# Separate tiles for messages and weighted values, reversed matmul order, and a query copy in a two-network graph kernel

## The chip, the cores and the metric

The kernel runs on one core of a Trainium2 chip. The metric is the device time of one launch in microseconds. A core has five engines that work side by side, each through its own queue in the order of the program: TensorE (PE, with its weight loads shown as PEld), VectorE (DVE), ScalarE (ACT), GpSimd (POOL) and SyncE (SP). An instruction that needs another engine's or a transfer's result waits for a semaphore, and everything behind it in the same queue waits too. Row gathers are issued by POOL, all other transfers that matter here by SP.

## The reference

A graph of N = 3125 nodes with 256 features has 53125 edges (`src`, `dst`), sorted by `dst`. Two networks follow each other, each added to its input and normalised:

```
h = x;  for each of 2 attention layers:
    q, k, v = h@wq+bq, h@wk+bk, h@wv+bv            # 4 heads of 64
    alpha   = sum(q[dst]*k[src]) / 8                # per edge and head
    alpha   = softmax of alpha over the edges of a dst
    h       = segment_sum(v[src]*alpha, dst) + h@ws + bs
    h       = leaky_relu(batch_norm(h))
x = layernorm(x + h)
h = x;  for each of 3 relational layers:
    msg = relu(h[src] * (edge_attr @ nn_w.T + nn_b))
    out = h@root + bias
    for r in 0..2: out += (mean of msg over a dst's edges of type r) @ W[r]
    h = out
out = layernorm(x + h)
```

## The kernel before

Edges, padded to 53248, lie in T = 416 tiles of 128, one edge per partition. A group is G = 8 tiles, and there are NG = 52 groups. A prologue prepares index tables and the first table of keys and values, then a branch leads to `sorted_edges` (its other side, for unsorted edges, is not taken). The order within each engine's queue is the order in which the Python program writes the instructions (`tc.manual_schedule()`). Tiles come from pools with a number of buffers; a new tile waits until the last reader of the buffer's former tile is done.

`gather` (L442) is one indirect transfer on POOL that fetches 128 rows by the indices `src_c`. Each pass over the edges has 416 of them, and there are five passes: two in `window_attention`, three in `window_relational`.

**Attention.** A loop over `it` from 0 to 51 is a software pipeline: in iteration `it`, `loads(it+3)` sends the query window of a later group (SP), `penalties(it+1)` and `windows(it+1)` prepare the next one (`windows` compares destinations with a ramp on DVE, L511), `queries` (L520, PE) spreads query rows to edges, `logits(it)` multiplies by the gathered keys and sums per head (L525, L527, DVE), `turn(it-1)` (L532, PE) and `maxima(it-2)` (two scans, L537 and L538, DVE) make running maxima, `less(it-2)` (L544 and L546, PE) subtracts them, `weights(it-2)` (L550) and `weigh(...)` (L558, ACT) take the exponential and scale the values, in place in the gathered tile `kvg`. `nodes_of(it-3)` (L568) makes eight one-hot tiles that tell each edge's node, `sums(it-4)` (L575, PE) multiplies them with the weighted values and `add(it-5)` (L586, DVE) adds the result to a per-node accumulator. `rows(it+2)` issues eight gathers at the end of an iteration. Once a block of nodes is complete, `finish` divides by the softmax's sum (L612), adds the skip product (`skip`, L617 and L619) and keeps the result (L623). After the loop the last three groups are drained, with one-hot tiles made on POOL (`nodes_of(..., GP)`) and part of the weighting on DVE (`weigh_rest`, L563). This drain is called a tail below. Then come batch statistics and, after the first layer, the projection of the second layer's keys and values (L418), or, after the second, the layer norm that writes the rows for the relational part.

**Relational.** A loop over `s` from 0 to 103 takes half a group, a four of tiles, per step. `rows` gathers a group ahead by four groups into `xs`, a ring of six groups; `edge_weights` (L943, PE) computes the edge factors, `messages` (L961 on DVE, then the ReLU L962 on ACT) works in place in `xs`; a column of ones behind each row of `xs` counts edges in the first layer. `keys` (L953) makes one-hot tiles of node and edge type, `products` (L969, PE) reduces four tiles in PSUM and `add` (L983) adds them to a ring of node blocks. A complete block goes through `node`: means (L997, and the block's reset L998), transposes (`turn`, L1012 and L1013), the product with four weight matrices (`product`, L1023) and the sum with the bias (L1028), which SP writes to the table for the next layer. A new layer's first gather waits until all rows of that table are written.

Of the kernel before, what the change touches and what calls it, by code (L numbers as in the profile page):

```python
# [8 lines left out]
F32 = mybir.dt.float32  # L9
# [3 lines left out]
AF = mybir.ActivationFunctionType  # L13
OP = mybir.AluOpType
# [4 lines left out]
P = 128  # L19
# [4 lines left out]
D = 256  # L24
H = 4
HD = D // H
HC = HD + 1
# [431 lines left out]
def window_attention(tc, A, h_tab, L):  # L459
# [7 lines left out]

    with tc.tile_pool(name="a1", bufs=1) as one, tc.tile_pool(name="kvf", bufs=6) as kp, \
            tc.tile_pool(name="a3", bufs=3) as sp, tc.tile_pool(name="a2", bufs=2) as sp2, \
# [13 lines left out]

        kvs, qws, lds, pns, ohts, qds, fs, ws, ohs, pos, tos = ({} for _ in range(11))


        def loads(n, g):
            ldb = sp.tile([P, 2 * P], F32, name="ldb")
            SY.dma_start(ldb, view(L["ld_d"], g * G * P, [[2 * P, 4], [0, W2], [1, 2 * P]]))
            qw = sp.tile([P, D], F32, name="qw")  # L490
            _, at = nc.values_load_multi_w_load_instructions(
                L["q_row"][:, g * 4:g * 4 + 4], engines=[SY.engine], min_val=0, max_val=N + 3,
                skip_runtime_bounds_check_because="a pair's first dst: a node, or one of the padding's")
            for a in range(4):
                SY.dma_start(qw[a * W2:(a + 1) * W2, :], q_tab[bass.ds(at[a], W2), :])
            lds[g], qws[g] = ldb, qw

# [11 lines left out]
        def windows(g):  # L509
            oht = sp2.tile([P, 2, P], F32, name="oht")  # L510
            V.tensor_scalar(oht.rearrange("p k e -> p (k e)"), lds.pop(g), L["wid"], None, op0=OP.is_equal)  # L511
            ohts[g] = oht

# [28 lines left out]
        def less(g):  # L542

            TE.matmul(less_p, ident, al[:, g * G + 1:g * G + G + 1, :].rearrange("p t h -> p (t h)"),  # L544
                      start=True, stop=False)
            TE.matmul(less_p, fs.pop(g)[:, 64:64 + P], neg, start=False, stop=True)  # L546

# [5 lines left out]
        def weigh(g, a, b):  # L553

            for j in range(a, b):
                for q in range(H):
                    c = kvs[g][:, j, D + q * HC:D + (q + 1) * HC]
                    S.activation(c, c, AF.Copy, scale=ws[g][:, j * H + q:j * H + q + 1])  # L558

        def weigh_rest(g, a):  # L560

            c = kvs[g][:, a:, D:].rearrange("p t (h c) -> p t h c", h=H)
            V.tensor_tensor(c, c, bc(ws[g][:, a * H:].rearrange("p (t h) -> p t h", h=H), 3, HC), op=OP.mult)  # L563

# [6 lines left out]
        def sums(g):  # L571
            oh, kv = ohs.pop(g), kvs.pop(g)
            po = qps.tile([P, AC], F32, name="pof")
            for j in range(G):
                TE.matmul(po, oh[:, j, :], kv[:, j, D:], start=(j == 0), stop=(j == G - 1))  # L575
            pos[g] = po
# [24 lines left out]
        def finish(i):  # L601
# [12 lines left out]
            def skip(p):  # L614
                for c in range(2):
                    for k in range(2):
                        TE.matmul(p[:, c, :], wqs[:, k, D + c * P:D + (c + 1) * P], xT[:, k, blk],  # L617
                                  start=(k == 0), stop=False)
                    TE.matmul(p[:, c, :], q["a"][:, c * P:(c + 1) * P], ident, start=False, stop=True)  # L619

            def keep(p):
                for c in range(2):
                    S.activation(xT[:, c, blk], p[:, c, :], AF.Identity, bias=cols[:, 0, c:c + 1])  # L623
# [252 lines left out]
def window_relational(tc, A, first, out, L):  # L876
# [8 lines left out]
    h = L["xT"].rearrange("p k n -> p (k n)")[:KM].rearrange("p (i c) -> p i c", c=D)  # L885
    NQ, XB, AB = 2 * NG, 6, 3

    with tc.tile_pool(name="rx", bufs=1) as one, tc.tile_pool(name="edf", bufs=3) as sp, \
            tc.tile_pool(name="atf", bufs=4) as wp, tc.tile_pool(name="rnf", bufs=2) as np_, \
            tc.tile_pool(name="edpf", bufs=2, space=PSUM) as ps, \  # L890
# [3 lines left out]
        rc = one.tile([KM, KT], F32, name="rck")  # L894
        xs = one.tile([P, XB, G, KW], F32, name="xsf")
        ab = one.tile([P, AB, G, 64], F32, name="abf")
        at_d = L["dram"].tile([NG, P, 4 * P], F32, name="at_d")
        V.memset(ab, 0.0)
        V.memset(ab[:, :, :, DD], 1.0)
        V.memset(xs[:, :, :, D], 1.0)  # L900

        ats, ohs, ews, pps, tos = {}, {}, {}, {}, {}

# [42 lines left out]
        def rows(g, table):  # L946
            for j in range(G):
                gather(xs[:, g % XB, j, :D], table[:, :], L["src_c"][:, g * G + j:g * G + j + 1])

# [6 lines left out]

        def messages(q):
            g, u = divmod(q, 2)
            x4 = xs[:, g % XB, 4 * u:4 * u + 4, :D]
            xk = x4.rearrange("p (a k) c -> p k a c", k=2)  # L960
            V.tensor_tensor(xk, ews.pop(q), xk, op=OP.mult)  # L961
            S.activation(x4, x4, AF.Relu)  # L962

        def products(n, q):
            g, u = divmod(q, 2)
            wide = D + (n == 0)
            pp = ps.tile([P, 2 * D], F32, name="ppf")[:KM, :KW]
            for j in range(4 * u, 4 * u + 4):
                TE.matmul(pp[:, :wide], ohs[g][:, j, :], xs[:, g % XB, j, :wide],  # L969
                          start=(j == 4 * u), stop=(j == 4 * u + 3))  # L970
            pps[q] = pp
# [13 lines left out]
        def node(n, i, nxt, w, bias):  # L985
# [18 lines left out]
            def turn(c):  # L1004
                if q["end"]:
                    if c == 0:
                        q["t"] = ps.tile([P, 2, 2, D], F32, name="ewf")
                    t = q["t"][:, c].rearrange("p a d -> p (a d)")
                else:
                    t = ps1.tile([P, 2 * D], F32, name="nodf")  # L1010
                for b in range(3):
                    TE.transpose(t[:, b * KM:(b + 1) * KM], q["k"][:, b, c * P:(c + 1) * P], ident[:KM, :KM])  # L1012
                TE.transpose(t[:, 3 * KM:4 * KM], h[:, i, c * P:(c + 1) * P], ident[:KM, :KM])  # L1013
                S.copy(q["m"][:, c, :R].rearrange("p r (b k) -> p b r k", b=3),
                       t[:, :3 * KM].rearrange("p (b r k) -> p b r k", b=3, r=R))
                S.copy(q["m"][:, c, R], t[:, 3 * KM:4 * KM])

            def product():
                pool, name = (ps, "ppf") if i == NT - 1 else (ps1, "nodf")
                q["o"] = pool.tile([P, 2 * D], F32, name=name)[:KM, :D]  # L1020
                for c in range(2):
                    for r in range(R + 1):
                        TE.matmul(q["o"], q["m"][:, c, r, :], w[:, r, c, :], start=(r + c == 0),  # L1023
                                  stop=(r == R and c == 1))

# [36 lines left out]
        for n in range(3):  # L1062
# [5 lines left out]
            for s in range(NQ):  # L1068
# [8 lines left out]
                if s + 1 < NQ:  # L1077
                    edge_weights(s + 1)
                messages(s)
                if s >= 2:  # L1080
# [693 lines left out]
```

## Time and profile before

| what | us |
|---|---|
| median of 9 runs (2959.47 to 2967.19) | 2965.18 |
| the profiled execution's own time | 2972.51 |
| its span | 2970.7 |
| mean granted TensorE clock | 0.876 |
| PE busy | 2473.0 (83%) |
| DVE busy | 2181.1 (73%) |
| POOL busy | 2032.5 (68%) |
| ACT busy | 1341.8 (45%) |
| 1248 relational gathers, busy | 1202.6 |
| 832 attention gathers, busy | 799.6 |

Busy time is the time in which an engine executes at least one instruction. "Idle before" a group of instructions is time in which its engine stood still directly ahead of them; the profile names what ended it, and "issue" where it sees nothing that was waited for. The chain is the sequence of work that ended last, followed back from the end. A group of a stretch's instructions is written as: start, duration, engine, line, operation, tiles written and read, shapes, number of instructions merged, and in brackets the idle time before it.

### The profile page before, as it was taken

How to read it: one execution, taken by the hardware profiler on the slowest of the kernel's cores; microseconds unless marked ns; L12 is line 12 of the kernel's file. 1: busy time of each engine (PE TensorE's matmuls, PEld its weight loads, DVE VectorE, ACT ScalarE, POOL GpSimd, SP SyncE). 2: the span in 40 equal slices, each digit the busy share in tenths (PEclk: the TensorE clock that was granted, in tenths of full speed). 3: DMA queues.
4: the chain of work that ended last, by engine and by line, in shares of the span. 5: the costliest groups of instructions: out<-in, count | busy, mean ns of one | idle time of the engine just before them, and what ended most of it. 6: DMA issues, size and time to landing. Idle time of an engine off the chain costs nothing.

```text
span 2970.7 us, 45198 instructions
## 1 busy us (share of the span) xinstructions
PE 2473.0 (83%) x12210; PEld 1823.8 (61%) x12210; DVE 2181.1 (73%) x5167; ACT 1341.8 (45%) x4207; POOL 2032.5 (68%) x2131
## 2 busy tenths in 40 slices
PE   6688888887888788849899988788898878988887
PEld 3366666663666666636667766466666656666665
DVE  5599999975899999866666665566666646777775
ACT  1388787861788788653332332122222212222222
POOL 0677777744777777537777775777777757777774
PEclk9688888887888888859999999799999979999998
DMA  4788888836888888555555553444444444444442
GB/s 131 236 263 247 247 243 242 238 101 216 252 245 247 245 240 242 163 160 163 150 149 147 147 150 103 138 140 139 135 131 140 131 124 132 147 139 147 137 145 84
DMA packets 290315, 517.96 MB, mean 174 GB/s; under 512 B 101389, under 2 KB 170394, under 8 KB 290054
## 3 DMA queue, kind: packets, MB, share of 16 engines
q0 software_dynamic: 126720, 383.94, 44.8%
q1 hardware_dynamic: 162902, 130.81, 14.5%
q8 instruction: 104, 1.70, 0.2%
q14 instruction: 158, 1.29, 0.1%
q10 hardware_dynamic: 431, 0.21, 0.0%
HBM read 468.08 MB, written 46.70 MB: 173 GB/s over the span
## 4 chain that ended last, share of the span: by engine, by line
PE 43%; DVE 17%; DMA 16%; issue 12%; POOL 9%; DVEq 1%; ACT 1%; SPq 0%; POOLq 0%; another core or an unknown queue 0%; ACTq 0%
PE ppf L969 14%; PE ewf L943 8%; DMA xsf<-h_tab,src_c 8%; POOL kvg L442 8%; PE nodf L1023 6%; DMA kvg<-kv_tab,src_c 6%; PE pof L575 4%; DVE xsf L961 3%; DVE kvg L525 2%; DVE ohkf L953 2%; PE qdf L520 2%; POOL xsf L442 2%; PE qdf L418 1%; PE partps L617 1%; DVE ohn L568 1%
## 5 line engine op out<-in xcount | busy, mean ns | idle before, releaser
L442 POOL DMA_INDIRECT xsf<-h_tab,src_c x1248 | 1202.6, 964 | 488.0 <-issue 274.6
L442 POOL DMA_INDIRECT kvg<-kv_tab,src_c x832 | 799.6, 961 | 325.1 <-issue 219.2
L558 ACT ACTIVATE kvg<-kvg,wts 128x65 f32<-128x65 f32 x3216 | 786.3, 336 | 3.5
L962 ACT ACTIVATE xsf<-xsf 128x1024 f32<-128x1024 f32 x312 | 329.9, 1058 | 1008.2 <-DVE xsf L961 1008.1
L961 DVE TENSOR_TENSOR xsf<-ewf,xsf 128x1024 f32<-128x1024 f32 x312 | 381.5, 1223 | 527.1 <-DMA xsf<-h_tab,src_c 322.1
L969 PE MATMUL ppf<-xsf,ohkf 128*126 128x256 f32 (+1 forms) x2496 | 702.3, 429 | 0.0
L969 PEld LDWEIGHTS ppf<-xsf,ohkf 128*126 128x126 f32 x2496 | 494.4, 208 | 182.3 <-issue 41.0
L943 PE MATMUL ewf<-nnwf,atw 33*128 33x256 f32 x2496 | 383.5, 430 | 163.2 <-DVE xsf L961 162.0
L575 PE MATMUL pof<-kvg,ohn 128*128 128x260 f32 x1664 | 434.6, 419 | 6.9 <-DVE ohn L568 3.2
L575 PEld LDWEIGHTS pof<-kvg,ohn 128*128 128x128 f32 x1664 | 338.1, 209 | 106.2 <-ACT kvg L558 22.6
L943 PEld LDWEIGHTS ewf<-nnwf,atw 33*128 33x128 f32 x2496 | 230.9, 200 | 272.7 <-DVE xsf L961 211.7
L525 DVE TENSOR_TENSOR kvg<-qdf,kvg 128x1024 f32<-128x1024 f32 x208 | 252.0, 1211 | 63.9 <-DMA kvg<-kv_tab,src_c 33.0
L1023 PE MATMUL nodf<-rwt,mts 128*126 128x256 f32 x1152 | 264.8, 383 | 0.0
L953 DVE TENSOR_SCALAR ohkf<-iotas,kr_c 128x126 f32<-128x126 f32 x1248 | 260.5, 295 | 0.0
L527 DVE TENSOR_REDUCE alf<-kvg 128x16 f32<-128x1024 f32 x208 | 253.8, 1220 | 7.1
L1023 PEld LDWEIGHTS nodf<-rwt,mts 128*126 128x126 f32 x1152 | 220.7, 192 | 34.3
L520 PE MATMUL qdf<-qw,oht 32*128 32x256 f32 x1664 | 201.3, 505 | 24.2 <-DVE kvg L525 8.6
L532 PE MATMUL soft<-identf,alf 128*32 128x128 f32 x312 | 59.0, 303 | 169.0 <-DVE fmax L537 163.9
L568 DVE TENSOR_SCALAR ohn<-iotas,nr_c 128x128 f32<-128x128 f32 x800 | 169.6, 300 | 0.0
L520 PEld LDWEIGHTS qdf<-qw,oht 32*128 32x128 f32 x1664 | 127.4, 239 | 67.9 <-issue 22.6
L983 DVE SCALAR_TENSOR_TENSOR kacc<-ppf,k_high,kacc 126x256 f32 (+1 forms) x312 | 151.2, 485 | 11.1
L550 ACT ACTIVATE wts<-soft 128x32 f32<-128x32 f32 x104 | 20.5, 198 | 295.9 <-PE soft L546 294.3
(223 smaller groups left out, 2148.8 us busy)
## 6 DMA issues: line engine op xcount, KB each, us to landing
atw<-at_d SPq DMA_DIRECT2D x104, 256.0 KB
xsf<-h_tab,src_c POOLq DMA_INDIRECT x1248
kvg<-kv_tab,src_c POOLq DMA_INDIRECT x832
ldb<-ld_rows SPq DMA_DIRECT2D x104, 128.0 KB
qw<-q_tab SPq DMA_DIRECT2D x416, 32.0 KB
at_d<-atw SPq DMA_DIRECT2D x52, 256.0 KB
abf<-in_edge_attr_dram SPq DMA_DIRECT2D x51, 128.0 KB
q_tab<-qs SPq DMA_DIRECT2D x50, 128.0 KB
```

Of the source, the lines that this page charges most:

```text
L442: return GP.indirect_dma_start(out=dst, out_offset=None, in_=table, in_offset=rows_of(idx))
L520: TE.matmul(qd[:, a, k, :], ohts[g][r, k, :], qws[g][r, :], start=True, stop=True)
L525: V.tensor_mul(kv, qds.pop((g, u)).rearrange("p a k c -> p (a k) c"), kv)
L527: V.tensor_reduce(al[:, t:t + 4, :], kv.rearrange("p t (h c) -> p t h c", h=H), AX.X, OP.add)
L558: S.activation(c, c, AF.Copy, scale=ws[g][:, j * H + q:j * H + q + 1])
L575: TE.matmul(po, oh[:, j, :], kv[:, j, D:], start=(j == 0), stop=(j == G - 1))
L943: TE.matmul(ew[:, k, a, :], ats[g][r, 2 * u + a, :], nnw[r, :], start=True, stop=True)
L953: V.tensor_scalar(oh[:, j, :], iota[:, :KM], L["kr_c"][:, g * G + j:g * G + j + 1], None, op0=OP.is_equal)
L961: V.tensor_tensor(xk, ews.pop(q), xk, op=OP.mult)
L962: S.activation(x4, x4, AF.Relu)
L969: TE.matmul(pp[:, :wide], ohs[g][:, j, :], xs[:, g % XB, j, :wide], start=(j == 4 * u), stop=(j == 4 * u + 3))
L1023: TE.matmul(q["o"], q["m"][:, c, r, :], w[:, r, c, :], start=(r + c == 0), stop=(r == R and c == 1))
```

## The change

- `messages` writes into a tile `msf` of its own (four buffers) and no longer in place; the ones come from a constant by a small ACT copy, in the first layer only. The gathered rows lie in twelve tiles `xsf` of four rows each instead of a ring of six groups, without the extra column.
- `weigh` and `weigh_rest` write into a tile `wvg` (two buffers) instead of in place in `kvg`, and `sums` reads it. `kvg` has five buffers instead of six.
- `sums`, `products`, `turn`, `product` and `keep` take their tiles, columns or relations last to first. `skip` starts with the divided block, `less` with the maxima, `turn` with the node's own row.
- `windows` copies the query rows on DVE into `qwc`, from which `queries` reads; `loads` sends the four transfers in reverse.

```diff
-            tc.tile_pool(name="kvf", bufs=6) as kp, \
+            tc.tile_pool(name="kvf", bufs=5) as kp, \
...
-            for a in range(4):
+            for a in reversed(range(4)):
                 SY.dma_start(qw[a * W2:(a + 1) * W2, :], q_tab[bass.ds(at[a], W2), :])
...
             V.tensor_scalar(oht.rearrange("p k e -> p (k e)"), lds.pop(g), L["wid"], None, op0=OP.is_equal)
-            ohts[g] = oht
+            qw = sp2.tile([P, D], F32, name="qwc")
+            V.tensor_copy(qw, qls.pop(g))
+            ohts[g], qws[g] = oht, qw
...
+            TE.matmul(less_p, fs.pop(g)[:, 64:64 + P], neg, start=True, stop=False)
             TE.matmul(less_p, ident, al[:, g * G + 1:g * G + G + 1, :].rearrange("p t h -> p (t h)"),
-                      start=True, stop=False)
-            TE.matmul(less_p, fs.pop(g)[:, 64:64 + P], neg, start=False, stop=True)
+                      start=False, stop=True)
...
+            if a == 0:
+                wvs[g] = sp2.tile([P, G, AC], F32, name="wvg")
...
-                    S.activation(c, c, AF.Copy, scale=ws[g][:, j * H + q:j * H + q + 1])
+                    S.activation(wvs[g][:, j, q * HC:(q + 1) * HC], kvs[g][:, j, D + q * HC:D + (q + 1) * HC], AF.Copy,
+                                 scale=ws[g][:, j * H + q:j * H + q + 1])
...
-            for j in range(G):
-                TE.matmul(po, oh[:, j, :], kv[:, j, D:], start=(j == 0), stop=(j == G - 1))
+            for j in reversed(range(G)):
+                TE.matmul(po, oh[:, j, :], kv[:, j, :], start=(j == G - 1), stop=(j == 0))
...
                 for c in range(2):
+                    TE.matmul(p[:, c, :], q["a"][:, c * P:(c + 1) * P], ident, start=True, stop=False)
                     for k in range(2):
                         TE.matmul(p[:, c, :], wqs[:, k, D + c * P:D + (c + 1) * P], xT[:, k, blk],
-                                  start=(k == 0), stop=False)
-                    TE.matmul(p[:, c, :], q["a"][:, c * P:(c + 1) * P], ident, start=False, stop=True)
+                                  start=False, stop=(k == 1))
...
         def rows(g, table):
-            for j in range(G):
-                gather(xs[:, g % XB, j, :D], table[:, :], L["src_c"][:, g * G + j:g * G + j + 1])
+            for q in (2 * g, 2 * g + 1):
+                xs[q] = xp.tile([P, 4, D], F32, name="xsf")
+                for j in range(4):
+                    gather(xs[q][:, j, :], table[:, :], L["src_c"][:, q * 4 + j:q * 4 + j + 1])
...
+        def messages(n, q):
+            ms[q] = wp.tile([P, 4, KW], F32, name="msf")
+            m = ms[q][:, :, :D]
+            by_rows = [x.rearrange("p (a k) c -> p k a c", k=2) for x in (m, xs.pop(q))]
+            V.tensor_tensor(by_rows[0], ews.pop(q), by_rows[1], op=OP.mult)
+            if n == 0:
+                S.copy(ms[q][:, :, D:], one4)
+            S.activation(m, m, AF.Relu)
...
-            for j in range(4 * u, 4 * u + 4):
-                TE.matmul(pp[:, :wide], ohs[g][:, j, :], xs[:, g % XB, j, :wide],
-                          start=(j == 4 * u), stop=(j == 4 * u + 3))
+            for j in reversed(range(4)):
+                TE.matmul(pp[:, :wide], ohs[g][:, 4 * u + j, :], ms[q][:, j, :wide], start=(j == 3), stop=(j == 0))
...
-                for b in range(3):
+                TE.transpose(t[:, 3 * KM:4 * KM], h[:, i, c * P:(c + 1) * P], ident[:KM, :KM])
+                for b in (2, 1, 0):
                     TE.transpose(t[:, b * KM:(b + 1) * KM], q["k"][:, b, c * P:(c + 1) * P], ident[:KM, :KM])
-                TE.transpose(t[:, 3 * KM:4 * KM], h[:, i, c * P:(c + 1) * P], ident[:KM, :KM])
...
-                for c in range(2):
-                    for r in range(R + 1):
+                for c in (1, 0):
+                    for r in reversed(range(R + 1)):
```

## The prediction

> **What bounds the kernel now.** I read the stages first, then the gathers, then what stands between the stages. The cuts of the first view are at the first and last row gather of each pass; its columns are length, then busy time (and instructions) of PE, PEld, DVE, ACT and POOL, then granted clock, DMA share and GB/s.
>
> ```profile
> 89.43:616.61 527.18, 429.38 (x2293) 326.84 (x2294) 469.40 (x965) 403.05 (x1659) 400.67 (x416) 0.83 0.84 246
> 616.61:700.65 84.04, 73.70 (x250) 43.91 (x248) 57.81 (x145) 29.09 (x84) 12.97 (x17) 0.96 0.26 96
> 700.65:1226.10 525.45, 426.16 (x2286) 326.54 (x2287) 467.96 (x961) 400.70 (x1657) 398.94 (x416) 0.83 0.84 245
> ...
> 1303.64:1833.35 529.71, 471.80 (x2379) 350.62 (x2380) 346.71 (x882) 169.05 (x248) 403.23 (x416) 0.91 0.56 156
> ...
> 1861.20:2387.90 526.70, 450.24 (x2160) 329.16 (x2161) 332.45 (x825) 133.74 (x195) 400.22 (x416) 0.91 0.45 136
> ...
> 2411.50:2937.10 525.60, 452.31 (x2154) 328.33 (x2155) 365.43 (x935) 141.43 (x217) 399.09 (x416) 0.90 0.48 142
> ```
>
> Five passes, two of attention and three relational, take 526 to 530 us each, although their work on PE, DVE and ACT differs widely. What they share is POOL: 416 gathers. A few of those, in attention and in a relational pass:
>
> ```profile
> 303.84 0.94 POOL L442 DMA_INDIRECT kvg<-kv_tab,src_c  x1 [0.30 <-issue]
> ...
> 305.09 0.95 POOL L442 DMA_INDIRECT kvg<-kv_tab,src_c  x1 [0.30 <-issue]
> ...
> 2003.12 1.01 POOL L442 DMA_INDIRECT xsf<-h_tab,src_c  x1 [0.30 <-issue]
> 2004.44 0.94 POOL L442 DMA_INDIRECT xsf<-h_tab,src_c  x1 [0.30 <-PE ppf L969]
> ```
>
> A gather starts every 1.25 us: 0.945 of work and 0.305 before the next. In the waits of POOL inside the passes none is longer than 0.3, whatever engine is named: POOL never stands still for data or a buffer. So a pass costs 416 x 1.25 = 520 us and the 6 to 10 us by which some gathers are longer than 0.945 (the profile's mean is 0.961 and 0.964). PE at 80 to 90% busy is in its shade. The other 335 us are the start (89), the two attention tails (84 and 78), the ends of relational passes (28 and 24) and the last tail (34). A change pays or costs only through the gather's period, or through the chain in a tail.
>
> Does a wait cost POOL time? Semaphore instructions at the gather line, first pass and then the relational ones:
>
> ```profile
> L442 POOLq EVENT_SEMAPHORE  x46: 17/17/17, 145.4 to 600.6; - x46
> ...
> L442 POOLq EVENT_SEMAPHORE  x1176: 17/17/34843, 1356.9 to 2928.9; - x196
> ```
>
> Nearly every relational gather has a second wait and needs an extra instruction of 17 ns; in attention 46 of 416 have one. The idle time between gathers is 0.30 in both. It lies inside that gap.
>
> **The change part by part**, as the instructions are ordered in both kernels.
>
> *Messages in their own tiles.* L962 and the products now use msf, and gathers wait for DVE's product instead of PE's. Gathers that wait on PE (1169 of 1248) become 298 that wait on DVE. Gain on POOL 0, by the comparison above. In the first relational pass 104 four-column copies on ACT are new: 0.27 us each by the small copies at L1016, 28 us, on an engine busy 169 of 530 us, placed while it waits for DVE (it waits 1008 us there). Cost 0; with that cover gone, 0.27 us at the end of that pass.
>
> *Products last to first.* Relational: one activation makes the four tiles, so nothing is later; 1248 products lose their gather wait. Of L575's 832 matmuls, 104 groups keep one waiting matmul each; the profile has 824 semaphore instructions of 56 ns on PE's queue there, 46 us. All this lies under POOL's period. In the tails the chain's pof groups take 3.51 us for 8 matmuls, 0.44 each, as they do without a break, so removed waits give 0 (end of the range: 2 us gained, some 0.4 in each of five tails).
>
> The reverse order has a price in attention: the first matmul of `sums` needs the last one-hot tile. In steady groups that delays PE by about 1.4 us (DVE's eight tiles take 1.7 to 1.9 us) but PE then waits for DVE anyway: 169 us before L532 in all, 3.4 us in the group at 304.5. Hidden, as long as DVE is no earlier. In the tails it shows. First tail:
>
> ```profile
> 618.51 12.97 POOL L568 TENSOR_SCALAR ohn<-iotas,nr_c 128x128 f32<-128x128 f32 x16 [1.90 <-PE pof L575]
> ...
> 631.23 3.67 PE L575 MATMUL pof<-kvg,ohn 128*128 128x260 f32 x16
> ```
>
> POOL's sixteen tiles end at 631.48, and PE began the group of the last eight at 631.23. POOL itself waited for the sums of group 47, whose first matmul (612.53) came 0.8 before its last tile was done (611.64 + 1.65 = 613.29); their end slips by 0.5 to 0.8, so POOL's end does, and the group starts at about 632.2: +1.0. Second tail, the same pattern:
>
> ```profile
> 1239.67 6.83 POOL L568 TENSOR_SCALAR ohn<-iotas,nr_c 128x128 f32<-128x128 f32 x8 [8.23 <-PE soft L532]
> ...
> 1245.86 1.48 PE L575 MATMUL pof<-kvg,ohn 128*128 128x260 f32 x6
> ```
>
> Group 48's sums slip 0.7, POOL's eight tiles end at 1247.2, PE starts at 1247.3 instead of 1245.86: +1.4.
>
> *`skip` with the divided block first.* In both tails PE had done one `wqs` pair before the division was ready and now does it behind it:
>
> ```profile
> 641.91 0.49 PE L619 MATMUL qdf<-identf,naf 128*128 128x128 f32 x2 [1.54 <-DVE naf L612]
> ...
> 642.23 0.61 PE L617 MATMUL qdf<-xT,wqs 128*128 128x128 f32 x4
> ```
>
> Half of an x4 group moves behind the wait, twice 0.22: +0.5 in each tail. Tails together: 1.0 + 1.4 + 0.5 + 0.5 = **+3.4 us**. Bounds: 0 if another wait already covers it, 6 if each of the three last `sums` in each tail slips a whole one-hot series less what is done (about 1.0). In `less`, L546 goes ahead of L544; the pair's end moves by 0.2 us in front of an activation with 4.6 us idle: 0. `keep` in reverse: before, too, the first activation waited for all of PE's group: 0.
>
> *Relational `turn` and `product`.* After the last DVE mean come three transposes instead of two: +0.15 us (0.49 for three) at three pass ends, **+0.4** (-0.5 to +1). The final product starts at 2404.50, its copies end at 2401.88, so needing the last copy first costs 0.
>
> *Queries copied on VectorE.* 104 new copies 128x256. The nearest row is L511, same shape, next instruction in the queue:
>
> ```profile
> L511 DVE TENSOR_SCALAR oht<-ldb,wid x104: 329/343/558, 108.9 to 1213.5; 128x256 f32<-128x256 f32 x104
> ```
>
> The next DVE instruction follows 0.26 us later (302.82 to 303.08), so 52 x 0.26 = 14 us of DVE per pass. DVE is busy 469 of 527 and spends the rest on waits and issue; attention's first group lags its gather by 20 us, which shrinks to 3 to 5 us by the middle of the pass, with idle moments from there on. Taking 0.26 off each idle moment in turn, the lag at the pass's end grows by 0.3 at most: 0 (up to +3). Behind the copy in the queue stand the accumulation, `logits` and so PE's next queries. The copy also waits for four query DMAs; they are issued two groups (20 us) ahead, and the SP queue sends them earlier than before, since the buffer is now freed by the copy, a group earlier than by PE. Only the first group of a pass has no lead: about 0.3 us, no gather waits for it. PE's L520 loses its 416 DMA waits, under the same shade.
>
> The copy can hold the gathers, though. In attention they exceed 0.945 us by 16 ns x 832 = 13.3 us. DVE instructions with one SBUF source that stand beside them are L568 and L511, 169.6 + 37.7 = 207 us busy, so 0.064 us held per us. The copies add some 37 us of that kind: **+2.4 us**. Upper bound: each holds POOL for its whole 0.26, 104 x 0.26 = 27. Lower bound: -3, since moved DVE work can also miss the gathers. I take 2.4, from the nearest rows.
>
> The Trainium skill speaks against this copy: SBUF — State Buffer, section Who interferes with whom, says that an fp32 copy from SBUF to SBUF uses both ports and that GpSimd, which generates such gathers' descriptors, blocks until it ends. By that rule taken whole the copies would cost up to 104 x 0.34 = 35 us (an estimate from the page and L511's duration), and the sum would be 39 instead of 6.2. L511, which that section puts in the same class, has not stopped gathers for anything near its length here.
>
> *Five buffers.* A gather into group g+5's tile now waits for ACT's weighting of group g (before: g+6's for its sums). ACT ends group 0 at 139.3 and the gather of group 5 would start at 141.0: 1.7 us spare, at most 1.3 of which the first copies and `less` use; later groups have 4 to 20 us. 0 (up to +1). The weighted tile has two buffers; its reuse waits for sums that PE does ahead of `less`, for which the weighting waits anyway: 0.
>
> **Sum:** 3.4 + 0.4 + 2.4 = +6.2 us. The profiled execution took 2972.51 us (span 2970.7 and 1.8 around it), 7.3 above the median of 2965.18; 2972.5 becomes 2978.7, the median **2971.4**, x1.0021. Measuring this kernel tells about 0.2% (5.9 us) from no change, so it stands at the edge.
>
> **Rivals.**
> 1. *Copies hold the gathers for their length* (for: L998, 0.56 us, is often beside gathers of 1.2 us; against: L511). 27 instead of 2.4: 2996; half of it 2983.
> 2. *DVE becomes attention's bound.* For: busy 89% with long chains. It needs over 0.5 us per group, twice the copy; at 0.6, with the lag's catch-up spent, +5 per pass: 2981.
> 3. *Faster, by gathers that are held less.* Gathers lose 13.3 us in attention and 19 ns x 1248 = 23.7 us in the relational passes. Message rows are now 1024 bytes apart instead of 1028 on arrival, so DVE's steps can shift against the gathers. If half of 23.7 goes, -12: 2959.5. It decides for not slower from 6.2 us, for over 0.2% faster from 12.1 us. Against: nothing there removes a DVE instruction.
> 4. *Nothing changes*: tails covered, copies harmless: 2965.
> 5. *PE paces, and 2500 waits fewer pay.* L969 has 429 ns and L1023, without waits, 383: 46 x 2496 = 115 us, 2850. Against: POOL's even 1.25 us. 1 in 50.
>
> **Numbers.** Forecast (+1 to +12) 0.48, about half of it over 5.9; rival 1 0.16, rival 2 0.08, rival 3 0.17 (0.13 of it beyond 0.2%), rival 4 0.09, rival 5 0.02. Slower 0.48 x 0.52 + 0.24 = 0.49; faster 0.15; same 0.36. The range takes in rival 3's half and most of rival 1: 2954 to 2992; the forecast's own is 2966 to 2977.
>
> **What would show it.** Passes of 526 to 531 us with a gap of 0.30; attention gathers at a mean of 0.963 to 0.967; attention tails 86 and 79 to 80 us; PE's first `sums` matmul after the last one-hot tile. A wait over 0.3 on POOL inside a pass, or attention gathers above 0.98, makes it wrong.

## The result and the profile after

The changed kernel takes 2971.67 us (median of 10 runs, 2967.14 to 2981.8) beside 2964.54 us for the kernel before (31 runs): ratio 1.0032, 95% interval 1.0024 to 1.0040. The medians differ by 7.1 us; the ratio, which is taken over all runs, makes it 9.5 us (7.1 to 11.9). The forecast was 2971.4, slower by about 0.2%. The profiled execution took 2976.4 us (span 2974.6), 4.7 above its median, while that of the kernel before was 8.0 above its own. Two spans that differ by 3.9 us while the medians differ by 7.1 warn that one profile of each can't settle where 7 us went. So I read the places here, and the sizes from eight more profiles further down.

The stages of the changed kernel, cut at the first and last row gather of each pass (columns as in the prediction's first view):

```profile
90.53:621.24 530.71, 421.87 (x2290) 317.60 (x2291) 480.58 (x1017) 401.60 (x1654) 401.72 (x416) 0.83 0.84 245
621.24:707.49 86.25, 76.06 (x252) 44.12 (x251) 57.97 (x145) 28.98 (x88) 11.81 (x17) 0.94 0.25 93
707.49:1235.23 527.74, 415.75 (x2278) 311.55 (x2279) 477.22 (x1013) 400.93 (x1653) 401.30 (x416) 0.85 0.84 244
1235.23:1313.34 78.11, 42.35 (x191) 32.95 (x189) 57.96 (x152) 40.79 (x108) 11.26 (x18) 0.72 0.28 86
1313.34:1841.78 528.44, 455.56 (x2379) 342.52 (x2380) 347.07 (x882) 178.41 (x352) 402.00 (x416) 0.93 0.58 156
...
1869.30:2393.86 524.56, 442.39 (x2156) 326.06 (x2157) 333.05 (x825) 133.47 (x195) 398.15 (x416) 0.91 0.46 137
...
2419.18:2943.28 524.10, 448.49 (x2162) 328.68 (x2163) 366.36 (x935) 141.09 (x217) 397.66 (x416) 0.90 0.48 142
```

The attention passes grew by 3.5 and 2.3 us and their tails by 2.2 and 0.6; the three relational passes shrank by 1.3, 2.1 and 1.5. The page's gather groups (busy, mean ns of one, idle before):

```profile
L442 POOL DMA_INDIRECT xsf<-h_tab,src_c x1248 | 1197.8, 960 | 488.9 <-issue 399.3
...
L442 POOL DMA_INDIRECT kvg<-kv_tab,src_c x832 | 803.0, 965 | 329.0 <-issue 227.3
```

And the semaphore instructions at the gather line:

```profile
L442 POOLq EVENT_SEMAPHORE  x427: 17/17/35112, 87.1 to 2931.2; - x143
```

832 attention gathers took 803.0 us instead of 799.6. The semaphore instructions fell from 1293 to 427 (all of the run), and the gap between two gathers stayed 0.30: removing the waits paid nothing, as costed. One gap is not 0.30. The timeline of ACT and POOL there, before and then after the change:

```profile
131.54 7.78 ACT L558 ACTIVATE kvg<-kvg,wts 128x65 f32<-128x65 f32 x32
...
140.04 0.95 POOL L442 DMA_INDIRECT kvg<-kv_tab,src_c  x1 [0.31 <-issue]
```

```profile
135.23 7.78 ACT L561 ACTIVATE wvg<-kvg,wts 128x65 f32<-128x65 f32 x32
...
139.51 0.94 POOL L442 DMA_INDIRECT kvg<-kv_tab,src_c  x1 [0.30 <-issue]
...
143.28 0.94 POOL L442 DMA_INDIRECT kvg<-kv_tab,src_c  x1 [2.83 <-ACT wvg L561]
```

The gather at 143.28 is the first of group 5. It waits until ACT has weighted group 0 (135.23 + 7.78 = 143.01), because with five buffers it writes into group 0's tile. The prediction saw 1.7 us to spare here, with that gather at 141.0. In the kernel before the first gather of group 5 starts at 140.04 and ACT ends group 0 at 139.32 (131.54 + 7.78), so the spare was 0.7: the row that the prediction took is the gather after it.

The two places in the tails that the prediction priced, after the change:

```profile
625.23 11.81 POOL L572 TENSOR_SCALAR ohn<-iotas,nr_c 128x128 f32<-128x128 f32 x16 [3.99 <-issue]
...
637.09 3.77 PE L579 MATMUL pof<-wvg,ohn 128*128 128x260 f32 x16
...
1250.05 6.49 POOL L572 TENSOR_SCALAR ohn<-iotas,nr_c 128x128 f32<-128x128 f32 x8 [7.50 <-PE soft L534]
...
1256.59 3.77 PE L579 MATMUL pof<-wvg,ohn 128*128 128x260 f32 x16
```

PE begins these sums when POOL's last one-hot tile is complete (625.23 + 11.81 = 637.04; 1250.05 + 6.49 = 1256.54), as the reversed order requires; before, it began 0.25 and 0.64 us ahead of that. Counted from the last gather of the pass, it begins 1.2 and 1.6 us later than before (15.85 for 14.62, 21.36 for 19.76); the prediction had 1.0 and 1.4.

### The profile page after: what moved, and what is told of

The parts are those of the page before. It is cut to its first block, busy times and chain, and to the rows that moved or that the text cites. A ratio compares the mean times of both kernels' runs of the same rounds, so it can differ in the third digit from the quotient of the medians.

```text
span 2974.6 us, 43134 instructions
## 1 busy us (share of the span) xinstructions
PE 2428.4 (82%) x12210; PEld 1786.6 (60%) x12210; DVE 2203.6 (74%) x5271; ACT 1350.4 (45%) x4311; POOL 2029.7 (68%) x2131
## 4 chain that ended last, share of the span: by engine, by line
POOL 21%; DMA 20%; DVE 19%; issue 19%; PE 17%; ACT 3%; DVEq 1%; SPq 0%; POOLq 0%; another core or an unknown queue 0%; ACTq 0%
DMA xsf<-h_tab,src_c 11%; POOL xsf L442 11%; POOL kvg L442 10%; DMA kvg<-kv_tab,src_c 6%; PE ppf L977 4%; DVE ohkf L959 4%; DVE kacc L990 3%; ACT wvg L561 2%; PE ewf L947 2%; DVE kvg L527 2%; PE nodf L1030 2%; PE pof L579 2%; DVE msf L967 1%; PE qdf L418 1%; DVE ohn L572 1%
## 5 line engine op out<-in xcount | busy, mean ns | idle before, releaser
L442 POOL DMA_INDIRECT kvg<-kv_tab,src_c x832 | 803.0, 965 | 329.0 <-issue 227.3
L561 ACT ACTIVATE wvg<-kvg,wts 128x65 f32<-128x65 f32 x3216 | 786.4, 336 | 3.6
L970 ACT ACTIVATE msf<-msf 128x1024 f32<-128x1024 f32 x312 | 330.0, 1058 | 990.5 <-DVE msf L967 988.1
L967 DVE TENSOR_TENSOR msf<-ewf,xsf 128x1024 f32<-128x1024 f32 x312 | 381.4, 1222 | 516.1 <-DMA xsf<-h_tab,src_c 366.5
L977 PE MATMUL ppf<-msf,ohkf 128*126 128x256 f32 (+1 forms) x2496 | 687.3, 423 | 0.6 <-DVE rsr L1049 0.5
L977 PEld LDWEIGHTS ppf<-msf,ohkf 128*126 128x126 f32 x2496 | 484.3, 204 | 178.0 <-issue 41.8
L579 PE MATMUL pof<-wvg,ohn 128*128 128x260 f32 x1664 | 446.2, 427 | 87.8 <-DVE ohn L572 63.9
L579 PEld LDWEIGHTS pof<-wvg,ohn 128*128 128x128 f32 x1664 | 347.1, 214 | 189.0 <-issue 81.8
L959 DVE TENSOR_SCALAR ohkf<-iotas,kr_c 128x126 f32<-128x126 f32 x1248 | 261.9, 296 | 0.1
L522 PE MATMUL qdf<-qwc,oht 32*128 32x256 f32 x1664 | 170.1, 477 | 27.0 <-DVE qwc L513 18.6
L572 DVE TENSOR_SCALAR ohn<-iotas,nr_c 128x128 f32<-128x128 f32 x800 | 168.9, 299 | 0.0
L990 DVE SCALAR_TENSOR_TENSOR kacc<-ppf,k_low,kacc 126x256 f32 (+1 forms) x312 | 148.4, 476 | 9.7 <-PE ppf L977 8.9
L522 PEld LDWEIGHTS qdf<-qwc,oht 32*128 32x128 f32 x1664 | 108.0, 223 | 63.2 <-issue 22.6
```

What stands on the lines that cost most here:

```text
L442: return GP.indirect_dma_start(out=dst, out_offset=None, in_=table, in_offset=rows_of(idx))
L522: TE.matmul(qd[:, a, k, :], ohts[g][r, k, :], qws[g][r, :], start=True, stop=True)
L561: S.activation(wvs[g][:, j, q * HC:(q + 1) * HC], kvs[g][:, j, D + q * HC:D + (q + 1) * HC], AF.Copy, scale=ws[g][:, j * H + q:j * H + q + 1])
L579: TE.matmul(po, oh[:, j, :], kv[:, j, :], start=(j == G - 1), stop=(j == 0))
L959: V.tensor_scalar(oh[:, j, :], iota[:, :KM], L["kr_c"][:, g * G + j:g * G + j + 1], None, op0=OP.is_equal)
L967: V.tensor_tensor(by_rows[0], ews.pop(q), by_rows[1], op=OP.mult)
```

## Experiments

Four sets, each timed beside the kernel before on the same chip. There the kernel before took 2965.04, 3655.95, 2964.75 and 2974.48 us; only ratios within a set are compared.

### Undoing parts of the change

Without the copy (`e1_no_copy`):

```diff
-            qw = sp2.tile([P, D], F32, name="qwc")
-            V.tensor_copy(qw, qls.pop(g))
-            ohts[g], qws[g] = oht, qw
+            ohts[g], qws[g] = oht, qls.pop(g)
```

> The changed kernel with the DVE copy of the queries taken out (queries read the four transfers' tile again); all else as changed. Theory A (the copy costs twice: it holds gathers, and as it waits for all four query transfers it delays DVE in the first two groups, which with five buffers blocks one gather for 2.83 us): that block goes, the attention gathers lose 13 to 14 us over 0.945 instead of 16.8, the median falls by about 6 us, 2971.7 to 2965 to 2966. Theory B (only the block is real, the gathers' 3.4 us is scatter of one profile): -2.8, about 2969. Theory C (five buffers block the gather whatever the copy does): the wait on ACT near 143 stays, change of the median under 1 us.

Measured: 2970.14 us, ratio 1.0015 (1.0005 to 1.0025). The gathers lose 14.1 us (800.3 of page time less 832 x 0.945), as theory A said, but the time didn't fall to its 2965 to 2966: without the copy the change still costs 4.4 us (1.5 to 7.4). The wait is still there, shorter:

```profile
138.65 0.94 POOL L442 DMA_INDIRECT kvg<-kv_tab,src_c  x1 [1.58 <-ACT wvg L559]
```

So the copy isn't its only cause. The first queries show another. In the kernel before PE started them 20.4 us after the first gather (109.79 - 89.43). Here, without any copy, it starts them 22.9 after (109.87 - 87.00). Before, then without the copy:

```profile
109.79 3.97 PE L520 MATMUL qdf<-qw,oht 32*128 32x256 f32 x16 [8.56 <-DVE oht L511]
```

```profile
109.87 2.11 PE L520 MATMUL qdf<-qw,oht 32*128 32x256 f32 x16 [9.52 <-DMA qw<-q_tab]
```

The four query transfers are sent in reverse, and PE's first matmul needs the one sent last. In the changed kernel DVE's copies delay the first multiplication further:

```profile
112.03 0.29 DVE L513 COPY qwc<-qw 128x256 f32<-128x256 f32 x1 [2.13 <-DMA qw<-q_tab]
...
117.10 0.29 DVE L513 COPY qwc<-qw 128x256 f32<-128x256 f32 x1 [2.05 <-DMA pn<-pen_rows]
117.40 1.22 DVE L527 TENSOR_TENSOR kvg<-qdf,kvg 128x1024 f32<-128x1024 f32 x1
```

The first multiplication stands behind the copy of group 1, before which DVE waits for a transfer (the profile names that of `pn`): it starts 26.9 us after the first gather (117.40 - 90.53), without the copy 25.7 (112.67 - 87.00), before the change 24.9 (114.35 - 89.43).

Direct reading in the first two groups only (`e2_direct_first`):

```diff
-            qw = sp2.tile([P, D], F32, name="qwc")
-            V.tensor_copy(qw, qls.pop(g))
+            qw = qls.pop(g)
+            if g > 1:
+                qc = sp2.tile([P, D], F32, name="qwc")
+                V.tensor_copy(qc, qw)
+                qw = qc
```

> The changed kernel, but the first two groups of each layer read the query transfers directly, and the other 50 still go through the copy. Theory A: the 2.83 us block at 143 goes, because DVE's first multiplication is back at 25 us after the first gather instead of 27; the gathers stay held by 16 to 17 us in the two attention passes; median -2.8, about 2969. Theory B: the same here. Theory C: the block stays, no change. If later copies also add lag, the block shrinks but some of it stays.

Measured: 2974.29 us, ratio 1.0036 (1.0023 to 1.0049; five runs). The wait shrank to 0.96 us, another of 1.08 us came at 168, and the gathers stayed at 802.9 us. The time didn't fall, so the runs give no sign that the wait in the first groups is what the change costs.

Sums and `skip` in the old order (`e3_forward`):

```diff
-            for j in reversed(range(G)):
-                TE.matmul(po, oh[:, j, :], kv[:, j, :], start=(j == G - 1), stop=(j == 0))
+            for j in range(G):
+                TE.matmul(po, oh[:, j, :], kv[:, j, :], start=(j == 0), stop=(j == G - 1))
```

> The changed kernel with sums first to last again and with skip's products in the old order. Theory A (the reversed order costs in the tails what the last one-hot tile is late): the two attention tails fall from 86.3 and 78.1 to about 84 and 77.5, passes unchanged, median -2.8 us, about 2969. Rival (the tails' difference lies elsewhere, in the copy or in the clock that PE was granted): tails stay at 86 and 78, change under 1 us.

Measured: tails 84.0 and 76.3 us as theory A said, but 2972.77 us, ratio 1.0034 (1.0022 to 1.0046; six runs). The interval doesn't exclude the 2.8 us, but gives no sign of them.

### One part alone

The relational part alone (`e4_rel_only`), the kernel before up to `window_relational` and the changed one from there:

```diff
-        xs = one.tile([P, XB, G, KW], F32, name="xsf")
...
+                xs[q] = xp.tile([P, 4, D], F32, name="xsf")
...
+            ms[q] = wp.tile([P, 4, KW], F32, name="msf")
```

> The kernel before with the relational part of the change alone (messages in a tile of their own, rows in twelve tiles 1024 bytes apart, products, turn and product in the new order). Theory A (gathers there are really held less: 18.5 us in the three passes instead of 23.2, and the end is 2 us shorter): -5 us against the kernel before, about 2959.5, ratio 0.998. Rival (scatter of one profile, the part is worth nothing): ratio 1.000 within 0.0005. Rival (the transposes' order costs in the gaps): +0.4.

Measured: 2965.96 us, ratio 1.0002 (0.9993 to 1.0011): no gain. Its relational gathers lose 20.3 us (1199.7 less 1248 x 0.945); the two other kernels with the old relational code that ran at the usual pace and left it alone lose 19.1 and 19.8. The profile of before, with 23.2, was the odd one.

The three attention parts alone ran first on a chip on which the kernel before took 3655.95 us, at a granted clock of 0.81 instead of 0.88. Why this chip is slower stays open.

Copy alone (`f1_copy_only`, and again as `g1_copy_only`):

```diff
+            qw = sp2.tile([P, D], F32, name="qwc")
+            V.tensor_copy(qw, qls.pop(g))
+            ohts[g], qws[g] = oht, qw
...
-            for a in range(4):
+            for a in reversed(range(4)):
```

> The kernel before, with the queries' copy on DVE and the reversed order of their four transfers alone; six buffers as before. Theory A (each copy holds a gather a little): the attention gathers lose 14 to 17 us over 0.945 instead of 10 to 13, no wait over 0.3 on POOL, since six buffers cover the late first groups; +3 to +4 us, ratio 1.0010 to 1.0014. Rival 1 of the prediction at half length: +13, ratio 1.0045. Rival (the copies are free and the loss lies in the buffers and the tails): under +1, ratio 1.000.

Measured there: 3656.66 us, ratio 1.0006 (0.9990 to 1.0023).

Orders alone (`f2_order_only`):

```diff
-            for j in range(G):
-                TE.matmul(po, oh[:, j, :], kv[:, j, D:], start=(j == 0), stop=(j == G - 1))
+            for j in reversed(range(G)):
+                TE.matmul(po, oh[:, j, :], kv[:, j, D:], start=(j == G - 1), stop=(j == 0))
```

> The kernel before, in place and with six buffers, with the attention's orders alone: sums last to first, skip and less with their late operand first, keep in reverse. Theory A: attention tails 86 and 78 to 79.5 instead of 84 and 76.5 to 77.5, passes unchanged, +3, ratio 1.0010. Rival (the waits removed from PE pay somewhere in the passes): ratio 0.999 or below. Rival (the tails only scatter): 1.000.

Measured there: 3716.47 us, ratio 1.0152 (1.0126 to 1.0179), with attention passes of 699 and 692 us against 663 and 658 with the copy alone. None of the expectations had that.

Tiles and five buffers alone (`f3_tiles_only`, and again as `g2_tiles_only`):

```diff
-            tc.tile_pool(name="kvf", bufs=6) as kp, \
+            tc.tile_pool(name="kvf", bufs=5) as kp, \
...
+                wvs[g] = sp2.tile([P, G, AC], F32, name="wvg")
```

> The kernel before, with five buffers for the gathered groups and the weighted values in a tile of their own, alone: no copy, sums forward. Theory A (five buffers block a gather near the start of the first attention pass even without the copy, 1.6 us in the run without copies): one or two waits on ACT over 0.3, 1 to 2 us together; +1 to +2, ratio 1.0005. Rival (ACT writing to another tile holds the gathers as well): attention gathers lose 16 us or more, +5. Rival (no effect; the 1.6 us belonged to another part): 1.000 and no such wait.

Measured there: 3844.80 us and, in the profiled run, 3868.91, which is 5.2% and 5.8% above the median of before; four more runs took 3915 to 3922 us. This is far outside all three expectations. On this chip POOL does stand still, with the copy alone for instance at the first gather of group 6, which needs a buffer:

```profile
184.31 0.95 POOL L442 DMA_INDIRECT kvg<-kv_tab,src_c  x1 [37.53 <-PE soft L534]
```

and with five buffers in many groups (waits of POOL in its first pass: us in total, times, longest):

```profile
POOL kvg L442 <- ACT wts L550: 154.3, 13, 12.5
...
POOL kvg L442 <- ACT wvg L559: 96.2, 12, 26.9
```

So these runs can't price what bounds the kernel where a gather leaves every 1.25 us. They show something else: where gathers wait for buffers anyway, the separate tile with one gather buffer fewer costs 5% or more and the attention's orders 1.5%. Which of the two, tile or buffer, the runs don't separate.

The two again at the usual pace:

> The kernel before with the queries' copy on DVE alone, again, where the kernel before should take about 2965 us so that POOL's gathers set the pace (on the chip that took 3656 us they did not). Theory A (each copy holds a gather by 0.03 to 0.04 us, as the attention gathers of three kernels with copies lose 16.6 to 16.8 us and those of three without 9.9 to 14.0): gathers lose 14 to 17 us, no wait over 0.3 on POOL, +3 to +4 us, ratio 1.0010 to 1.0014. Rival (the copy alone costs nothing, only together with five buffers): ratio within 0.0005 of 1 although gathers may be longer. Rival (half its length each): 1.0045.

> The kernel before with five buffers and the weighted values in a tile of their own alone, again where gathers set the pace. Theory A: one or two waits on ACT near the start of the first attention pass, 1 to 2 us in all, none in the second pass; +1 to +2 us, ratio 1.0004 to 1.0007. Rival (five buffers leave so little room that gathers wait in many groups, as on the slower chip, where this cost 7%): waits of 2 to 5 us in more than ten groups, ratio over 1.01. Rival (nothing): 1.0000 and no wait.

Measured: copy alone 2971.78 us, ratio **1.0019** (1.0010 to 1.0028), which is +5.6 us (3.0 to 8.3; the medians differ by 7.0). This run has the reversed transfers too, as its edit shows. Tiles and five buffers alone 2965.12 us, ratio **0.9996** (0.9987 to 1.0005), and no wait at group 5. The page's gather groups, copy alone first:

```profile
L442 POOL DMA_INDIRECT kvg<-kv_tab,src_c x832 | 803.4, 966 | 326.8 <-issue 222.5
```

```profile
L442 POOL DMA_INDIRECT kvg<-kv_tab,src_c x832 | 798.1, 959 | 327.4 <-issue 217.0
```

POOL waits up to 0.11 us longer than the usual 0.30 before five gathers with the copy alone; the rest of its cost that a row shows is in the gathers' own duration.

### The price of a copy, and what holds a gather

The probe for the price of a copy, 624 of them in the relational passes (`f4_copies_rel` on the slow chip, `g4_copies_rel` again):

```diff
             V.tensor_tensor(xk, ews.pop(q), xk, op=OP.mult)
+            for _ in range(2):
+                V.tensor_copy(cp[:, 1, :], cp[:, 0, :])
```

> The kernel before, with 624 more DVE copies 128x256 from one SBUF tile to another, two behind each product of a half group in the relational passes, where DVE is busy 330 to 365 of 527 us. Nothing reads them. It prices one copy's hold on gathers. By the prediction's 0.064 us held per us of copy (0.29 to 0.34 us each): +12 us, 0.02 per copy. By what attention shows after the change (3.4 to 4.3 us for 104 copies): +20 to +26. If each held a gather for its length: 180 us or more. If copies are free: under +3, with the gathers' mean at 0.957 to 0.964 as before.

> The kernel before with 624 more DVE copies 128x256 in the relational passes, two behind each product of a half group, again where gathers set the pace. It prices a copy. By the prediction's 0.064 us held per us (0.29 us each): +12 us, ratio 1.004. By the two moments of a gather (the attention copies account for 4.4 to 6.4 us of lengthening per 104, 0.043 to 0.062 each): +27 to +38, ratio 1.009 to 1.013. By the median of the copy alone (7.0 us for 104, with some of it lag): up to +42, ratio 1.014. If each held a gather for its length: +180.

Measured: 3661.89 us, ratio 1.0014 (0.9998 to 1.0029), and 2975.48 us, ratio **1.0006** (0.9997 to 1.0015): +1.8 us (-0.9 to 4.5) for 624 copies. Every price expected was too high, my 0.064 rule among them (+12); only the first list's last entry, under +3 if copies are free, held.

```profile
L442 POOL DMA_INDIRECT xsf<-h_tab,src_c x1248 | 1204.0, 965 | 490.2 <-issue 262.1
...
L965 DVE COPY cpf<-cpf 128x256 f32<-128x256 f32 x624 | 195.1, 313 | 10.8
```

With 195 us of copies the gathers are longer by 1 to 6 us (1204.0 against 1202.6, 1198.5 and 1199.2 in three profiles with the same relational code and no copies there). How a copy holds a gather in attention, one gather of the changed kernel shows:

```profile
1141.50 0.35 DVE L511 TENSOR_SCALAR oht<-ldb,wid 128x256 f32<-128x256 f32 x1
1141.54 1.33 POOL L442 DMA_INDIRECT kvg<-kv_tab,src_c  x1 [0.30 <-issue]
...
1141.76 0.29 DVE L513 COPY qwc<-qw 128x256 f32<-128x256 f32 x1
...
1143.17 0.95 POOL L442 DMA_INDIRECT kvg<-kv_tab,src_c  x1 [0.30 <-issue]
```

`oht` runs when the gather begins, the copy follows without a break and ends at 1142.05, and the gather ends 0.82 us after that, at 1142.87. This is the pattern: of the 277 lengthened gathers in the changed kernel (0.985 us or more) 73% end 0.80 to 0.85 us after the end of a DVE instruction, of 1784 gathers of normal length 5%; in the kernel before 80% and 4%. So a gather has a moment, some 0.12 us after its start (0.945 less 0.82), at which such an instruction holds it until that ends. A second, smaller cluster ends 0.10 to 0.15 us after the end of a DVE instruction: 14% of the lengthened gathers against 4% of the normal ones in the changed kernel, mostly after resets (L1005) and copies. Some lengthened gathers, most of them in attention, fit neither.

Away from the first moment a copy mostly leaves the gather as it is: of the probe's 141 copies that ran at it 66 stand so before the end of a lengthened gather; of 186 that ran 0.82 us after a gather's start one ran in a lengthened gather. Late in a gather it is the copy that waits: those that begin 0.50 to 0.55 us into a gather take 0.52 us (median), those that begin 0.30 to 0.45 us into it 0.28.

In attention the copy comes right behind L511 and prolongs its hold. In the four profiles with copies 13 to 25 gathers end 0.80 to 0.85 us after a copy and 1 to 6 after L511, and another 6 to 11 end 0.10 to 0.15 us after a copy; in the six without, 8 to 15 end 0.80 to 0.85 us after L511. So 22 to 30% of the attention copies hold a gather, of the probe's 624 copies 11%. The probe's copies also push other instructions off the moment: the one-hot tiles there (L955) stand so before the end of 65 lengthened gathers, in the three profiles with the same relational code and no copies there 93 to 113. The price of a copy is thus not its length; it goes by where it falls and by what it moves. The other hits come from the one-hot tiles (L959, L572 in the changed kernel), the resets of blocks (L1005), the division (L616) and L511.

The reset moved to ACT (`h1_reset_on_act`) was to test this and to gain from it:

```diff
-                V.tensor_single_scalar(a3, a3, -1.0, op=OP.is_lt)
+                S.activation(a3, a3, AF.Copy, scale=0.0)
```

> The kernel before, with the reset of finished blocks in the relational passes (L998, 75 instructions of 0.56 us) moved from DVE to ACT, as a multiplication by zero. The hold on gathers goes by single moments: in the traces so far a lengthened gather ends either 0.82 us or 0.125 us after the end of a DVE instruction of a one-source kind that lay beside it, and L998 and its likes account for 8.8 to 10.9 us of the lengthening per execution (9.3 in the kernel before). Theory A (the holder is the DVE instruction): relational gathers lose 9 to 14 us over 0.945 instead of 16.7 to 23.2, no lengthened gather ends so beside ACT's instruction; -6 to -9 us, ratio 0.997 to 0.998. Rival (any long write to that memory holds gathers, whichever engine does it): no change in the gathers, ratio 1.000 or up to 1.001. Rival (DVE's next accumulation waits for ACT and the ends of the passes grow): gathers shorter, gaps between passes longer by 0.5 to 1 each, ratio 0.999.

Measured: 2973.68 us, ratio 1.0003 (0.9994 to 1.0012): nothing gained. That the holder is the DVE instruction came true: none of ACT's 75 resets (0.85 us each) stands 0.80 to 0.85 or 0.10 to 0.15 us before a gather's end, and the 43 gathers that had one running 0.125 us after their start took 0.945 to 0.951 us. In the kernel before, 23 of the 41 gathers with a DVE reset at that moment were lengthened. So the rival of any long write is out. The size fell short, relational gathers losing 15.5 us (1194.9 of page time) where 9 to 14 were expected, since the one-hot tiles of L953 now stand so before the end of 146 lengthened gathers instead of 113; the passes took 524.7 to 525.0 us. The rest was given back at the ends of the passes (29.4, 28.6 and 37.1 us, against 27.2, 24.7 and 33.2 with the tiles alone), by ACT's queue:

```profile
1837.32 0.88 DVE L997 TENSOR_SCALAR mk<-kacc,rck 126x256 f32<-126x256 f32 x3
1838.23 0.84 ACT L998 ACTIVATE kacc<-kacc 126x771 f32<-126x771 f32 x1 [3.51 <-DVE mk L997]
1838.98 0.46 ACT L1014 COPY mts<-ewf 128x378 f32<-128x378 f32 x1
1839.34 0.27 ACT L1016 COPY mts<-ewf 128x126 f32<-128x126 f32 x1
1839.66 0.50 PEld L1012 LDWEIGHTS ewf<-identf,mk 126*128 126x128 f32 x3 [4.51 <-ACT mts L1016]
```

The reset of the last block waits for that block's means, and the copies of the block before stand behind it, though PE had finished their transposes at 1835.38. Resetting on ACT except for the last two blocks of a pass was not run.

### All profiles at the usual pace

Worked out from the traces; "over" is a group's gather time on the page less 0.945 us each, the last column POOL's waits of over 0.32 us in the first attention pass.

| kernel | attention over | relational over | first tail | second tail | waits |
|---|---|---|---|---|---|
| before | 13.4 | 23.2 | 84.0 | 77.5 | none |
| tiles only | 11.9 | 19.8 | 85.3 | 77.8 | none |
| relational part only | 9.9 | 20.3 | 85.0 | 76.3 | 1.31 |
| reset on ACT | 14.0 | 15.5 | 84.2 | 75.8 | 0.63 |
| copies in the relational passes | 14.7 | 24.6 | 83.6 | 77.2 | 3.43 |
| changed, no copy | 14.1 | 19.7 | 86.1 | 79.7 | 1.58 |
| changed, direct in the first groups | 16.7 | 16.6 | 85.9 | 75.6 | 0.96, 1.08 |
| changed, sums forward | 16.8 | 17.5 | 84.0 | 76.3 | 2.37 |
| copy only | 17.2 | 19.1 | 84.6 | 76.5 | five of 0.35 to 0.41 |
| changed | 16.8 | 18.4 | 86.3 | 78.1 | 2.83 |

## Why the prediction was right, and where it was not

The median was right to 0.3 us, and that is partly luck: by the ratio of all runs the change costs 9.5 us (7.1 to 11.9) where the sum had 6.2, and the terms were less exact still. The copy was sized at less than half, and the prediction's own sign of being wrong, a wait over 0.3 on POOL inside a pass, came.

- **Copies, +2.4 by held gathers: they do hold gathers, but the term was sized too low.** In the four profiles with attention copies the gathers lose 16.7 to 17.2 us, in the six without 9.9 to 14.7 (mean 13.0): +3.9. The step that failed is "0.064 us held per us" as a rate; the probe had 195 us of copies at 0.03 us held per us or less and no clear cost. The copy with the reversed transfers costs 5.6 us (3.0 to 8.3); taking only the copy out of the changed kernel brings the ratio from 1.0032 to 1.0015, which is 5 us. What it costs beyond the 3.9 of gathers is within its interval and isn't settled.
- **Rival 1 (held for the copy's length, 13 to 27 us) is refuted** by the upper end of 8.3. So is the 35 us that the prediction estimated from the Trainium skill, SBUF — State Buffer, section Who interferes with whom. That section says that whichever of the two issues first has the shared ports for its whole instruction, while the other blocks. The traces agree that a copy can hold a gather until it ends, and a gather a copy (0.52 us instead of 0.28); they don't agree that it is for the whole instruction, as copies that begin 0.30 to 0.45 us into a gather run at 0.28.
- **First groups "about 0.3 us, no gather waits for it" and "1.7 us spare": wrong.** The spare was 0.7 us, less than the 1.3 that the prediction itself set against it. And I costed the reversed transfers at nothing. They and the copies make the first groups later (first queries by 1.5 and 2.5 us, first multiplication by 2.0 in the changed kernel), and the first gather of group 5 waited in all four kernels with reversed transfers and five buffers (0.96 to 2.83). With five buffers alone it did not. But single waits of 0.6 to 3.4 us also stand in three kernels with the old attention and six buffers, near 190 to 213, so "POOL never stands still" was true of one profile, not of the kernel. Against these the change's waits cost perhaps 1 us (an estimate: 2.2 us on average in its four kernels, 1.3 in the four with the old attention and six buffers). Removing most of them left the time where it was (`e2_direct_first`).
- **Tails, +1.5 and +1.9: the first right, the second not resolved.** Reversed: 86.3, 86.1, 85.9; forward: 83.6 to 85.3, mean 84.4 of seven; so +1.7. The second tail has 78.1, 79.7 and 75.6 against 75.8 to 77.8, mean 76.8: +1.0 with a scatter of 2. PE begins after the last one-hot tile in both, 1.2 and 1.6 us later where 1.0 and 1.4 were forecast. That they cost this in the median is not shown: the kernel with the old order was no faster.
- **Waits removed, 0: right.** 866 fewer semaphore instructions on POOL, the same 0.30 gap; tiles alone 0.9996, relational part 1.0002. Rival 5 (PE paces) is out.
- **Rival 3 (gathers held less in the relational passes, -12): refuted.** The two profiles show 4.8 us less, but the relational part alone brings nothing in the median, and the table has 19.1 and 19.8 beside the 23.2 for the old code, 16.6 to 20.3 for the new. The spacing of rows is no lever here.
- **`turn`, +0.4, and ACT's copies of ones, 0:** not contradicted by the 1.0002 (0.9993 to 1.0011) of that part, which can't resolve 0.4 us.
- **Rival 2 (DVE becomes the bound): not seen.** DVE's busy time rose by 9 to 11 us a pass, and POOL's wait is that of the first groups alone. **Rival 4 (nothing changes)** is out, as the ratio's interval begins at 1.0024.

Sum of the terms as the profiles give them: 3.9 (gathers) + 1.7 and 1.0 (tails) + about 1 (waits) = 7.6, against 7.1 by the medians and 9.5 by the ratio. These terms are differences between profiles that scatter by several microseconds, so the sum is no proof. The timed runs say this much: the copy with the reversed transfers costs 5.6 us (3.0 to 8.3), everything but the copy together 4.4 (1.5 to 7.4). Alone, the tiles with five buffers and the relational part cost nothing, so these 4.4 us lie with the attention's orders, the reversed transfers (with five buffers they make a gather wait), or parts acting together. How they divide stays open; the attention's orders alone were not run where gathers set the pace.

## What to carry to other kernels

Compare several profiles before giving a few microseconds to a place: two of the same code differed by 4 us in their gathers alone. Price an instruction beside another engine's work by where it falls against that work and by what it displaces, not by its length. And when a change both delays the start of a pipeline and takes one of its buffers, cost the two together, for each may be hidden alone.

## What was not expected of the hardware

- A row gather of 0.945 us is sensitive to DVE about 0.12 us after its start: it then goes on when the DVE instruction ends and takes 0.82 us more. A second, smaller cluster ends 0.10 to 0.15 us after a DVE instruction. An ACT instruction of 0.85 us at the first moment left the gather at 0.945 to 0.951 us. 624 copies of 0.31 us cost 1.8 us (-0.9 to 4.5), 104 at a worse place 5.6 (3.0 to 8.3).
- Chips differ: the same kernel before took 2965, 2974 and 3656 us. On the slowest, gathers found no free buffer (37.5 us at the first gather of group 6), and a separate tile with a buffer less cost 5% or more where it cost nothing elsewhere.
